# The feed-forward of the L2 attention by pairs of sequences, and the keys and values of the L3 attention made early and kept in DRAM

## The chip, the cores and the metric

The kernel is one program on one core of a Trainium2 chip. Its engines run side by side, each through its own queue in order: PE (TensorE, the matmuls; PEld are its weight loads), DVE (VectorE), ACT (ScalarE), POOL (GpSimd) and SP (SyncE, which here only starts DMA transfers). An engine waits for another by semaphores. The metric is the device time of the program in microseconds (us), lower is better, and a comparison goes by the median of several runs.

## The reference, cut to what matters

The input x holds 8 sequences of 128 rows and 128 channels in fp32; ctx_1024 holds 77 context rows for each sequence. Eight blocks are added to x one after the other: L0_xattn, L0_ffn, L1_xattn, L1_ffn (64 routed experts, the best 3 for each row), L2_xattn, L2_ffn (six layers of windowed local attention), L3_xattn, L3_ffn (two such layers). The change touches these three:

```python
x = x + _L1_ffn_ref(_layernorm(x), ...)                     # experts
# L2_xattn: 16 heads of 8 channels, then a feed-forward of 512, both with a norm behind them
q, k, v = query @ Wq + bq, context @ Wk + bk, context @ Wv + bv
o = softmax(rope(q) @ rope(k).T / sqrt(8)) @ v @ Wo + bo
x = _layernorm(query + o, g1, b1)
ff = relu(x @ W1 + bf1) @ W2 + bf2
x = _layernorm(x + ff, g2, b2)
...
# L2_ffn, each of six layers: shift, QKV, norm of q and k, rotation, windowed softmax, Wo, gated feed-forward
# L3_xattn: 8 heads of 64 channels; y is the context, so k and v depend on no layer before it
xn = _layer_norm(x, ln_scale, ln_bias)
q, (k, v) = xn @ Wq, split(y @ Wkv)
out = softmax(q @ k.T / 8) @ v @ Wo
```

A sequence depends on no other sequence in all of this (only the routing of the experts looks across them).

## The kernel before, in words

The program has two parts, each a list of steps that a planner in the program's builder puts in order. A step names the engines that may do it with a guessed time for each, the tiles it reads and writes, and the kind of buffer it opens ("big" is 128x512 fp32, "row" 128x128, "mm" one of the 8 PSUM banks). `Plan.arranged` (line 599) plays the steps through with these guesses and writes down for each engine a fixed order; on the chip only this order and the semaphores are left. A step may be picked only while its rank is less than 600 (`AHEAD`) above that of the first step not yet started; steps of SP are free of this limit (line 639). So which tile a buffer number holds, and where an instruction stands in its queue, is decided by the planner.

**The front part** (`plan_front`, line 971) holds L0, L1_xattn and the experts. SP loads the packs of weights first and then, as 51 big buffers allow (`BUFS_A`, line 966), the weights of the 64 experts, 128 tiles of 256 KB, 38 of them before it has to wait for the routed rows (`rows_in`, line 1380), 90 behind them. Each expert's result goes to DRAM (`expert_ys`).

**The later part** (`plan_later`, line 2038) begins with the gathers: for each of the 8 sequences POOL starts three indirect transfers out of `expert_ys` (line 1464) and DVE adds each to x with its gate (line 1469). Behind them `one(b)` (line 1538) does the L2 attention of one sequence: a norm (DVE statistics L775 and L777; four POOL instructions L768, L782, L783, L784 for the root; ACT L792), a transpose (L754), two projections and a rotation (L761, L1501, L1505), scores (L847), exponentials (L855), sums and outputs (L863), a reciprocal (L869), the projection (L883, L884) and the sum `y` (L1550).

`layer(h)` (line 1555) then does the feed-forward of L2_xattn for a half, four sequences at once: norm, the affine step on POOL (`affine`, L1601 and L1602), transposes, four matmuls of 512 columns (L761) with ReLU (L1572 on ACT or L1574 on DVE), 4x5 small matmuls (L1582, L1584), a sum (L1588), a second norm and affine step, and the sum into x on POOL (L1594). `begin(l2, h)` (line 1690) makes the normed input `y_res` of the local layers for these four.

A local layer (class `Local`) takes one sequence at a time. `first` makes the shifted transposed input `hs` of a half (`shifted`, line 1743) and then queries and keys: matmuls L1757, the rotation on DVE (L1779, L1781, L1783) and POOL (L1784, L1797), the inverse root with Ln and Exp on ACT (L1810, L1811). `rest` does the attention (scores L1862 and L1868, exponentials L1875, sums and outputs L1923 and L1929, Ln and Exp again at L1883 and L1884, projection L1843, sum into `y_res` L1847). `gated` (line 1938), a gated feed-forward over a half, ends a layer: it opens with a matmul that shifts rows (L1944), goes on with L1961, L1974 and L1984, and leaves ACT with the table of Ln and Exp together (`preload_act_table_set`, L1969).

The order in which `plan_later` writes the steps: `one` for sequences 0 to 3; the loads of the first local weights and of the pack `w3`, all held behind the gathers of sequence 3 (`route.behind(3, ...)`); `layer(0)`, `begin(l2, 0)`; then `one` for 4 to 7 side by side with the first local layer of 0 to 3; `layer(1)`, `begin(l2, 1)`, `gated(l2, 0, 0)`, and so on, half by half through six layers. Beside the local attention of the last half-layers stands L3_xattn (`plan_xattn_64`, line 1605): for each half four matmuls make the transposed keys (128 context columns of four sequences, 308 columns), and for each sequence one matmul makes the values (77x512), all from `ctxT` and the part `L3_kv` of the pack `w3`. Each result is copied out of PSUM into a big buffer (L741 on ACT, L743 on DVE).

At the very end a flag decides by a branch whether a slower general version must run; here it never does.

Of the kernel before, what the change touches and what calls it, by code (L numbers as in the profile page):

```python
# [25 lines left out]
B = 8  # L26
# [109 lines left out]
def laid_out(i):  # L136
# [54 lines left out]
    w3.add("L3_kv", i["L3_xattn_Wkv"])  # L191
    w3.add("L3_o", chunked(i["L3_xattn_Wo"]))

    def local(m, qkv, wo, a, b):
        rest = [np.concatenate([chunked(o), with_unit(u), chunked(padded_rows(np.concatenate([d, e[None]]), 3 * P))], 1)
                for o, u, d, e in zip(i[m + wo], i[m + a], i[m + b], i[m + "b2"])]
# [12 lines left out]
        "wg": wg.array(), "w": w.array(), "w3": w3.array(),  # L209
# [4 lines left out]
                    "w": w.at, "w3": w3.at}  # L214
# [5 lines left out]
class Chip:  # L220


    def __init__(self, ctx, tc, a, at):
# [8 lines left out]
        for name in ("col", "row", "cst", "wg", "w"):  # L232
            self.room(name, self.keep)
# [290 lines left out]
class Step:  # L524
    def __init__(self, rank, ns, emit, mode, tail, spare):
        self.rank, self.ns, self.emit, self.mode, self.tail, self.spare = rank, ns, emit, mode, tail, spare
        self.wants, self.gives, self.vals, self.opens = 0, [], [], []
        self.ready, self.start, self.engine = 0.0, None, None


class Plan:
# [32 lines left out]
    def add(self, ns, emit, reads=(), writes=(), mode=None, opens=(), tail=None, spare=0):  # L564


        s = Step(len(self.steps), ns, emit, mode, tail, spare)
# [31 lines left out]
    def arranged(self):  # L599
# [22 lines left out]
        while times:  # L622
# [8 lines left out]
            for e in free:  # L631
# [3 lines left out]
                while came[e]:  # L635
                    rank, s = heapq.heappop(came[e])
                    if s.start is not None:
                        continue
                    if (rank < first + self.AHEAD or e == "SP") and held.isdisjoint(v.tag for v in s.opens) and open_to(s):
                        pick = s  # L640
                        break
                    tags = [v.tag for v in s.opens]
                    held.update(k for k in ("mm",) if tags.count(k) > 1)
                    kept.append((rank, s))
# [321 lines left out]
BUFS_A = {"tiny": 30, "few": 3, "row": 6, "big": 51, "huge": 3, "w": 1, "wr": 1}  # L966
# [4 lines left out]
def plan_front(w, early, dram, wide, narrow):  # L971
# [41 lines left out]
    pack("w", 3000)  # L1013
    for e in range(EARLY):
        route.weights(e)
# [517 lines left out]
def plan_l2_xattn(w, ctx, route):  # L1533
# [21 lines left out]
    def layer(h):  # L1555
        xs, y = w.xs[4 * h : 4 * h + 4], [ys[4 * h + j] for j in range(4)]
        y1 = w.tile([P, 4, P])
        w.normed(lambda k, y1=y1: y1()[:, k, :], lambda k, y=y: y[k](), y, [y1])
        affine(w, y1, "L2_xattn_g1", "L2_xattn_b1")
        yT = w.tile([P, 4, P])  # L1560
        tp = w.turn(lambda k, y1=y1: y1()[:, k, :], [y1])
        w.copy(yT, tp, [tp], [yT], 591, 682)
        hs = []
        for k in range(4):
            ps, hT = w.bank([P, 4 * P]), w.tile([P, 4 * P])
            w.mm(ps, lambda k=k: c.get("w", "L2_W1", k * P, P), lambda yT=yT: yT().rearrange("p b s -> p (b s)"), [yT], [ps],
                 860)
# [8 lines left out]
            plan.add({"ACT": 597, "DVE": 683}, relu, [ps], [hT])  # L1576
            hs.append(hT)
        out, y2 = w.bank([P, 4, P]), w.tile([P, 4, P])
        for j in range(4):
# [8 lines left out]
        plan.add({"DVE": 683}, lambda e, y1=y1, y2=y2, out=out: nc.vector.tensor_tensor(y2(), y1(), out(), ALU.add),  # L1588
                 [y1, out], [y2])
        y3 = w.tile([P, 4, P])  # L1590
        w.normed(lambda k, y3=y3: y3()[:, k, :], lambda k, y2=y2: y2()[:, k, :], [y2], [y3])
        affine(w, y3, "L2_xattn_g2", "L2_xattn_b2")
        xv = c.x[:, 4 * h : 4 * h + 4, :]
        plan.add({"POOL": 1270}, lambda e, y3=y3, xv=xv: nc.gpsimd.tensor_tensor(xv, xv, y3(), ALU.add), [y3, *xs], xs)  # L1594
# [4 lines left out]
def affine(w, v, g, b):  # L1599
    c, nc = w.c, w.c.nc  # L1600
    w.plan.add({"POOL": 1270}, lambda e: nc.gpsimd.tensor_tensor(v(), v(), spread(c.get("row", g), 4, 1), ALU.mult), [v], [v])  # L1601
    w.plan.add({"POOL": 1270}, lambda e: nc.gpsimd.tensor_tensor(v(), v(), spread(c.get("row", b), 4, 1), ALU.add), [v], [v])  # L1602


def plan_xattn_64(w, nch, wq, wkv, wo, gamma, beta, bias, finish):
# [12 lines left out]

    def group(h, g, xT):
        qTs, kTs = [], []  # L1620
        for k in range(4 * g, 4 * g + 4):
            ps, kT = w.bank([P, 4, KC]), w.tile([P, 4, KC])
            w.mm(lambda ps=ps: ps().rearrange("p b k -> p (b k)"), lambda k=k: wkv[:, k * P : (k + 1) * P],
                 lambda: c.ctxT[:, h * 4 * KC : (h + 1) * 4 * KC], [], [ps], 520, opens=[kT])
            w.copy(kT, ps, [ps], [kT], 430, 470)
            kTs.append(kT)
# [14 lines left out]
        for j in range(4):  # L1641
            b = 4 * h + j
            ps, v = w.bank([KC, 512]), w.tile([KC, 512])
            w.mm(ps, lambda b=b: c.ctxT[:, b * KC : (b + 1) * KC],
                 lambda: wkv[:, inner + g * 512 : inner + (g + 1) * 512], [], [ps], 860, opens=[v])
            w.copy(v, ps, [ps], [v], 591, 682)
            finish(b, w.attend_64(qTs, j * P, kTs, j, v, wo[:, 4 * g : 4 * g + 4, :],
# [4 lines left out]
    return half  # L1652


def plan_l3_xattn(w):
    c, nc = w.c, w.c.nc

    def finish(b, out):
# [3 lines left out]
    return plan_xattn_64(w, 4, c.get("w3", "L3_q"), c.get("w3", "L3_kv"), c.get("w3", "L3_o").rearrange("p (c d) -> p c d", d=P),  # L1662
                         c.get("col", "L3_xattn_ln_scale"), c.get("col", "L3_xattn_ln_bias"), None, finish)


AHEAD = 1
BUFS_C = {"w": 2, "wr": 2, "tiny": 24, "few": 12, "row": 20, "big": 48}


class Local:  # L1670
# [4 lines left out]
    def __init__(self, w, name, depth, nch, window, wa, wb, room, wo=None):  # L1675
# [12 lines left out]
        self.layers, self.hs, self.begun = {}, {}, {}  # L1688

    def begin(self, h):  # L1690
        at = slice(4 * h, 4 * h + 4)
        self.w.normed(lambda k: self.y[:, 4 * h + k, :], lambda k: self.c.x[:, 4 * h + k, :], self.w.xs[at], self.ys[at])

    def first(self, l, h, j):
# [3 lines left out]
        if j == 0:  # L1698
            self.hs[h] = self.shifted(h)
        self.begun[l, h, j] = self.queries_keys(self.layers[l], self.hs[h], j)  # L1700

    def rest(self, l, h, j):

        self.attention(self.layers[l], 4 * h + j, self.hs[h], j, *self.begun.pop((l, h, j)))
# [38 lines left out]
    def shifted(self, h):  # L1743

        nc, plan = self.c.nc, self.plan
        hs = self.tile([P, 4, P])
        y = self.y
        tp = self.turn(lambda k: y[:, 4 * h + k, :], self.ys[4 * h : 4 * h + 4])
        plan.add({"POOL": 150}, lambda e: nc.gpsimd.memset(hs()[64:128, :, 0:1], 0.0), [], [hs])
        self.copy(lambda: hs()[0:64], lambda: tp()[0:64], [tp], [hs])  # L1750
        self.copy(lambda: hs()[64:128, :, 1:P], lambda: tp()[64:128, :, 0 : P - 1], [tp], [hs])
# [286 lines left out]
def plan_later(w, route, l2x, l2, l3x, l3, stored):  # L2038


    order = [(loc, l, h, j) for loc, depth in ((l2, 6), (l3, 2)) for l in range(depth) for h in range(2) for j in range(4)]
# [3 lines left out]
    def some(n):  # L2045

        for i in range(n):
            while at["first"] < min(at["rest"] + 1 + AHEAD, len(order)) and order[at["first"]][:3] in given:
                loc, l, h, j = order[at["first"]]
                loc.first(l, h, j)  # L2050
                at["first"] += 1
            loc, l, h, j = order[at["rest"]]
            loc.rest(l, h, j)
# [13 lines left out]
    def begin(loc, h):  # L2067
        loc.begin(h)
        given.add((loc, 0, h))

    def gated(loc, l, h):
        loc.gated(l, 4 * h, 4)
        given.add((loc, l + 1, h))

    one, layer = l2x
    side_by_side(each(one, range(4)))

    behind = lambda load: route.behind(3, load)
    l2.layers[0] = l2.weights(0, [w.xs[3]], behind)
# [118 lines left out]
```

## Time and profile before

| what | us |
|---|---|
| three runs without the profiler | 1550.05, 1552.71, 1555.53 (median 1552.71) |
| the profiled execution, its own device time | 1561.18 |
| its span, first to last instruction | 1559.4 |
| PE busy / DVE / ACT / POOL | 1425.1 / 920.4 / 936.9 / 816.6 |
| last matmul of the experts ends | 395.3 |
| first gather starts / last gather starts | 398.4 / 449.5 |
| first matmul of the local layers (L1757) | 486.9 |
| first L1944 (layer 0, first half) / second L1944 (second half) | 571.7 / 653.1 |
| keys of L3_xattn: first half / second half | 1238.6 to 1242 / 1315.4 to 1318 |

How to read it: the profile gives for each engine its busy time and what ended each idle stretch in front of an instruction; for PE also the clock that was granted, as a part of full speed. The stage that the change is about lies between 395 and 653 us, the time from the end of the experts to the moment when all 8 sequences have their first local layer's attention behind them. A view of "windows" gives each engine's busy time in a stretch that one chooses, with the count of its instructions; a "timeline" gives them one after the other.

### The profile page before, as it was taken

Reading aid. Unit: us, or ns where it says so; the run is one execution under the profiler, and the core shown is the slowest. Engines: PE = TensorE matmul, PEld = TensorE weight load, DVE = VectorE, ACT = ScalarE, POOL = GpSimd, SP = SyncE. Lnnn points to the kernel's source line nnn. Section 1 sums busy time; section 2 is a strip of 40 time slices with the busy share of each in tenths; the row PEclk is TensorE's granted clock in tenths of the full one; section 3 lists DMA queues with packets and bytes.
Section 4 is the critical chain, followed back from the end, with each engine's and each line's share of the span. In section 5 each row is a group of like instructions: output and inputs, shape, how many; then the busy total and the mean of one; then the engine's idle time right before and its main releaser. Section 6 shows DMA issues by size and latency. Waiting matters only on the chain.

```text
span 1559.4 us, 39024 instructions
## 1 busy us (share of the span) xinstructions
PE 1425.1 (91%) x16007; PEld 972.3 (62%) x16007; DVE 920.4 (59%) x1995; ACT 936.9 (60%) x1917; POOL 816.6 (52%) x1243
## 2 busy tenths in 40 slices
PE   7999998598587869999999999999999999899996
PEld 4777775375363555675666766667666667475654
DVE  5543764523356428668577585766857665657563
ACT  3676564253245846666666666666666676566764
POOL 3310225310566727777595674956749572536561
PEclk7999999699697989999999999999999999999997
DMA  9300001388301000100100010010000000000000
GB/s 335 131 1 21 8 2 42 111 296 324 124 21 69 1 1 1 56 16 2 42 16 15 2 56 16 1 49 23 2 22 22 2 22 2 21 2 1 1 2 16
DMA packets 39964, 74.00 MB, mean 47 GB/s; under 512 B 4102, under 2 KB 18630, under 8 KB 38496
## 3 DMA queue, kind: packets, MB, share of 16 engines
q1 hardware_dynamic: 33888, 66.16, 12.3%
q0 software_dynamic: 1536, 3.15, 0.6%
q8 instruction: 128, 2.10, 0.5%
q10 hardware_dynamic: 4352, 2.10, 0.5%
q14 instruction: 60, 0.49, 0.1%
HBM read 65.10 MB, written 6.29 MB: 46 GB/s over the span
## 4 chain that ended last, share of the span: by engine, by line
PE 59%; DVE 19%; ACT 8%; POOL 7%; issue 4%; DMA 2%; another core or an unknown queue 0%; ACTq 0%; SPq 0%; POOLq 0%; DVEq 0%
PE mm L1757 8%; PE mm L754 7%; PE mm L761 5%; PE mm L1843 5%; DVE big L1779 4%; DVE big L1781 4%; DVE few L1783 4%; PE mm L1868 3%; PE mm L1929 3%; PE mm L1984 3%; PE mm L1961 2%; PE mm L1974 2%; PE mm L863 2%; PE mm L1189 2%; PE mm L1175 2%
## 5 line engine op out<-in xcount | busy, mean ns | idle before, releaser
L741 ACT COPY big<-mm 128x512 f32<-128x512 f32 (+4 forms) x512 | 276.4, 565 | 222.0 <-PE mm L754 118.0
L1784 POOL TENSOR_TENSOR big<-big,big 128x512 f32<-128x512 f32 x224 | 283.8, 1275 | 237.1 <-DVE big L1781 232.0
L1757 PE MATMUL mm<-wide,big 128*128 128x512 f32 x672 | 323.5, 611 | 13.1 <-ACT big L741 10.6
L1797 POOL TENSOR_TENSOR big<-big,few 128x512 f32<-128x512 f32 x224 | 226.8, 1042 | 1.6
L754 PE MATMUL mm<-ident,big 128*128 128x128 f32 (+1 forms) x1430 | 206.4, 280 | 19.5 <-ACT big L792 4.4
L754 PEld LDWEIGHTS mm<-ident,big 128*128 128x128 f32 (+1 forms) x1430 | 162.7, 143 | 96.8 <-POOL big L1797 31.9
L1757 PEld LDWEIGHTS mm<-wide,big 128*128 128x128 f32 x672 | 120.0, 194 | 116.3 <-issue 83.9
L1779 DVE TENSOR_TENSOR big<-mm,big 128x512 f32<-128x512 f32 x224 | 152.4, 680 | 64.0 <-ACT big L1778 61.0
L1778 ACT ACTIVATE big<-mm 128x512 f32<-128x512 f32 x224 | 133.0, 597 | 91.0 <-PE mm L1757 83.5
L1781 DVE TENSOR_TENSOR big<-mm,big 128x512 f32<-128x512 f32 x224 | 152.4, 680 | 5.3 <-ACT big L1778 5.3
L1783 DVE TENSOR_REDUCE few<-big 128x8 f32<-128x512 f32 x224 | 151.0, 674 | 6.5 <-ACT big L1778 6.5
L1875 ACT ACTIVATE big<-mm 128x512 f32<-128x512 f32 x224 | 118.2, 610 | 34.4 <-PE mm L1868 34.4
L1843 PE MATMUL mm<-narrow,big 128*128 128x128 f32 x896 | 117.2, 283 | 11.6 <-DVE big L1891 11.3
L1843 PEld LDWEIGHTS mm<-narrow,big 128*128 128x128 f32 x896 | 108.6, 196 | 28.3 <-DVE big L1891 17.9
L1885 DVE TENSOR_TENSOR mm<-mm,big 128x512 f32<-128x512 f32 x64 | 44.5, 696 | 132.0 <-ACT big L1884 130.5
L1929 PEld LDWEIGHTS mm<-big,big 128*32 128x32 f32 x3072 | 86.7, 110 | 27.9 <-issue 27.2
L1868 PE MATMUL mm<-big,big 64*64 64x64 f32 (+2 forms) x3584 | 100.4, 238 | 1.2 <-ACT big L741 1.2
L1868 PEld LDWEIGHTS mm<-big,big 64*64 64x64 f32 x3584 | 94.2, 133 | 6.3 <-ACT big L741 2.0
L1929 PE MATMUL mm<-big,big 128*32 128x128 f32 x3072 | 94.1, 273 | 0.1
L822 POOL TENSOR_TENSOR big<-big,tiny 128x308 f32<-128x308 f32 x40 | 27.9, 700 | 97.3 <-DVE tiny L819 47.2
L1891 DVE SCALAR_TENSOR_TENSOR big<-mm,big 128x512 f32<-128x512 f32 x112 | 73.1, 686 | 5.6 <-PE mm L1929 0.4
L743 DVE COPY big<-mm 77x512 f32<-77x512 f32 (+2 forms) x74 | 47.6, 656 | 29.7 <-PE mm L1189 9.1
(277 smaller groups left out, 2335.4 us busy)
## 6 DMA issues: line engine op xcount, KB each, us to landing
big<-in_experts_dram SPq DMA_DIRECT2D x128, 256.0 KB, 4.9
wide<-in_l2a_dram SPq DMA_DIRECT2D x6, 1536.0 KB, 6.6
narrow<-in_l2b_dram SPq DMA_DIRECT2D x6, 534.0 KB, 3.5
narrow<-in_l2o_dram SPq DMA_DIRECT2D x6, 512.0 KB, 3.6
p_w<-in_w_dram SPq DMA_DIRECT2D x1, 2048.0 KB
expert_rows<-big SPq DMA_DIRECT2D x8, 256.0 KB, 13.9
big<-expert_rows SPq DMA_DIRECT2D x8, 256.0 KB, 3.8
expert_ys<-big ACTq DMA_DIRECT2D x16, 128.0 KB, 4.3
```

The source lines that it names most:

```text
L741: nc.scalar.copy(out(), in_())
L754: nc.tensor.transpose(tp()[:, k, :], v(k), c.ident)
L1757: self.plan.add({"PE": 860}, lambda e: nc.tensor.matmul(ps(), lhsT=hs()[:, j, :], rhs=wqkv()[:, o : o + 512], start=True, stop=True), [hs, ...
L1778: yield lambda e: nc.scalar.activation(sq(), heads(), AF.Square)
L1779: yield lambda e: nc.vector.tensor_tensor(t1(), heads(), spread(rot()[:, 2 * kind, :], 8, 1), ALU.mult)
L1781: yield lambda e: nc.vector.tensor_tensor(halves(t2()), halves(heads())[:, :, ::-1, :], sin(), ALU.mult)
L1783: yield lambda e: nc.vector.tensor_reduce(ss()[:, lo : lo + 8], sq(), AX.X, ALU.add)
L1784: yield lambda e: nc.gpsimd.tensor_tensor(t1(), t1(), t2(), ALU.add)
L1797: plan.add({"POOL": 1062}, lambda e, t=t, t1=t1, i=i: nc.gpsimd.tensor_tensor(t(), t1(), spread(r()[:, 8 * i : 8 * i + 8], 64, 2), ALU.mul ...
L1843: nc.tensor.matmul(out(), lhsT=oT()[:, k, :], rhs=wo()[:, 4 * g + k, :], start=(g == 0 and k == 0), stop=(4 * g + k == nch - 1))
L1868: nc.tensor.matmul(sc[s]()[at : at + 64, k, q:end], lhsT=kT()[lo : lo + 64, k, at : at + 64], rhs=qT()[lo : lo + 64, k, q:end], start=Fals ...
L1929: nc.tensor.matmul(avs[half]()[32 * t : 32 * t + 32, k, :], lhsT=vs[t // 2]()[:, at : at + 32], rhs=prs[t]()[:, k, :], start=True, stop=True)
```

## The change

Four things are done, all by the order and the size of steps; the sums computed are the same.

1. `layer` and `begin` work on any run of sequences, and `plan_later` calls them for pairs: `one` for 0 and 1, `layer` and `begin` for 0 and 1, then 2 and 3, and so on. In the first local layer the shifted input too is made by pairs. All four pairs stand before the first local attention in the written order, and `gated(l2, 0, 0)` stands behind the attention of all of sequences 0 to 3 as before.
2. The 8 key and 8 value tiles of L3_xattn are made at the start of the later part (`ahead`), written to 16 DRAM tiles (`Kept.put`, behind the gathers of sequence 1) and read back into big buffers where L3_xattn needs them (`Kept.get`). The reads may be started up to 300 ranks ahead (`within`).
3. The part `L3_kv` becomes a pack of its own, `w3kv` (128x1024, 512 KB), which stays in SBUF from the front part on and is loaded there before the experts' weights; the front's big buffers go from 51 to 49 for it.
4. The loads of the first local weights and of `w3` are held behind the gathers of sequence 1 and not 3.

```diff
-BUFS_A = {"tiny": 30, "few": 3, "row": 6, "big": 51, "huge": 3, "w": 1, "wr": 1}
+BUFS_A = {"tiny": 30, "few": 3, "row": 6, "big": 49, "huge": 3, "w": 1, "wr": 1}
...
     pack("w", 3000)
+    pack("w3kv", 1700)
     for e in range(EARLY):
         route.weights(e)
...
-    def layer(h):
-        xs, y = w.xs[4 * h : 4 * h + 4], [ys[4 * h + j] for j in range(4)]
-        y1 = w.tile([P, 4, P])
+    def layer(b0, n):
+        xs, y = w.xs[b0 : b0 + n], [ys[b0 + j] for j in range(n)]
+        y1 = w.tile([P, n, P])
...
+def affine(w, v, g, b, n):
+    nc = w.c.nc
+    for name, op in ((g, ALU.mult), (b, ALU.add)):
+        w.plan.add({"POOL": 80 + 300 * n}, lambda e, name=name, op=op: nc.gpsimd.tensor_tensor(
+            v(), v(), spread(w.c.get("row", name), n, 1), op), [v], [v])
...
+    def keys(h, k):
+        ps, kT = w.bank([P, 4, KC]), w.tile([P, 4, KC])
+        w.mm(lambda: ps().rearrange("p b k -> p (b k)"), lambda: wkv[:, k * P : (k + 1) * P],
+             lambda: c.ctxT[:, h * 4 * KC : (h + 1) * 4 * KC], [], [ps], 520, opens=[kT])
+        w.copy(kT, ps, [ps], [kT], 430, 470)
+        return kT
+
+    def values(b, g):
+        ps, v = w.bank([KC, 512]), w.tile([KC, 512])
+        w.mm(ps, lambda: c.ctxT[:, b * KC : (b + 1) * KC], lambda: wkv[:, inner + g * 512 : inner + (g + 1) * 512], [], [ps],
+             860, opens=[v])
+        w.copy(v, ps, [ps], [v], 591, 682)
+        return v
+
+    def ahead():
+
+        return [v for h in range(2) for v in (*(keys(h, k) for k in range(nch)), *(values(4 * h + j, 0) for j in range(4)))]
...
+class Kept:
+
+
+    def __init__(self, w, dram, name, n):
+        self.w, self.rooms, self.there = w, [dram.tile([P, 512], F32, name=f"{name}{i}") for i in range(n)], []
+
+    def put(self, vs, after, begun):
+        for v, room in zip(vs, self.rooms):
+            there = self.w.plan.fixed(None)
+            n = lambda v=v: int(np.prod(v().shape[1:]))
+            self.there.append(there)
+            self.w.plan.add({"SP": 500}, lambda e, v=v, room=room, n=n: begun(
+                self.w.c.nc.sync.dma_start(room[: v().shape[0], 0 : n()], self.flat(v()))), [v, *after], [there])
...
+    def get(self, shape, i):
+        v = self.w.tile(shape)
+        self.w.plan.add({"SP": 500}, lambda e: self.w.c.nc.sync.dma_start(
+            self.flat(v()), self.rooms[i][: shape[0], 0 : int(np.prod(shape[1:]))]), [self.there[i]], [v], within=300)
+        return v
...
-    one, layer = l2x
-    side_by_side(each(one, range(4)))
-
-    behind = lambda load: route.behind(3, load)
-    l2.layers[0] = l2.weights(0, [w.xs[3]], behind)
-    w.plan.add({"SP": 5000}, lambda e: behind(w.c.load("w3")), [w.xs[3]], [])
-    layer(0)
-    begin(l2, 0)
-    side_by_side(each(one, range(4, 8)), some(4))
+    (one, layer), (l3x, ahead, kept) = l2x, l3x
+    ahead = ahead()
+    for k in range(4):
+        side_by_side(each(one, (2 * k, 2 * k + 1)))
+        if k == 0:
+
+            behind = lambda transfer: route.behind(1, transfer)
+            kept.put(ahead, [w.xs[1]], behind)
+            l2.layers[0] = l2.weights(0, [w.xs[1]], behind)
+            w.plan.add({"SP": 5000}, lambda e: behind(w.c.load("w3")), [w.xs[1]], [])
+        layer(2 * k, 2)
+        begin(l2, 2 * k, 2)
+    side_by_side(some(4))
     plan_flag(w)
-    layer(1)
-    begin(l2, 1)
     gated(l2, 0, 0)
```

## The prediction

> **What bounds the kernel now.** I read the busy shares by slice first, then windows at the edges of the stage that is edited, then the chain of waits and single instructions there.
>
> ```profile
> PE   7999998598587869999999999999999999899996
> PEclk7999999699697989999999999999999999999997
> ...
> 395.30:408.90 13.60, 0.00 (x0) 0.00 (x0) 3.49 (x11) 0.86 (x2) 8.25 (x12) 0.55 0.15 43
> ...
> 486.90:571.70 84.80, 71.78 (x800) 47.51 (x800) 43.60 (x80) 60.00 (x95) 48.07 (x66) 0.93 0.01 1
> 571.70:600.00 28.30, 21.70 (x68) 11.42 (x69) 16.52 (x40) 14.84 (x28) 11.94 (x21) 0.82 0.00 1
> 600.00:653.10 53.10, 52.50 (x763) 37.04 (x762) 36.38 (x62) 36.45 (x73) 45.35 (x63) 1.00 0.09 32
> 653.10:1238.00 584.90, 580.58 (x7145) 387.17 (x7147) 406.22 (x732) 394.78 (x758) 394.64 (x543) 1.00 0.06 20
> 1238.00:1316.00 78.00, 76.73 (x1041) 53.80 (x1030) 45.36 (x99) 52.29 (x115) 42.55 (x65) 1.00 0.04 12
> 1316.00:1344.70 28.70, 24.01 (x129) 14.80 (x128) 14.18 (x41) 16.05 (x34) 8.27 (x15) 0.94 0.08 29
> ```
>
> Behind the length of a window stand the busy times of PE, PEld, DVE, ACT and POOL, then PE's clock and the DMA share. From 600 to 1316 PE is busy over 98% at full clock: there the time is PE's work, and whatever work PE is relieved of, or has done sooner, comes off the end. From 395.3 (the experts' last matmul) to 653.1 (the second L1944) PE is idle for 51.9 of 257.8 us, and part of the rest runs at a lower clock. That stage is bound by waits:
>
> ```profile
> 398.42 1.01 POOL row L1464
> ...
> 447.78 1.05 POOL tiny L782
> 449.48 1.09 POOL row L1464
> ...
> 480.00 1.04 POOL tiny L782
> 481.90 1.04 POOL tiny L782
> 484.01 1.64 PE mm L754 x4
> 486.89 9.83 PE mm L1757 x20
> 497.35 1.28 ACT L1810
> 498.89 1.28 ACT L1811
> ```
>
> These are pieces of the chain: gathers and roots on POOL, one feed-forward of four sequences from 444 to 487 in which PE has little beside it, then local attention that needs Ln and Exp in turn, each time with a table load of 1.28 us on ACT.
>
> **The landmark.** I compared the order in which the changed program issues its instructions. From the experts' end to the second L1944 its PE queue holds what it held, with W1 split into twice as many matmuls of half the width, plus the 16 matmuls for keys and values; behind it, only these 16 are missing. So the change is worth (a) the shift of the second L1944, (b) the missing work after it, (c) side costs. The sum is made against the profiled execution, 1561.2 us (span 1559.4); that is 8.5 us or 0.5% above the median of the runs, 1552.7, and I take the same difference off both.
>
> **Keys and values, early.** Eight matmuls of 308 columns, 0.52 us apart at 1315.4 to 1316.4, and eight of 512 columns, 0.86 apart: 8 x 0.52 + 8 x 0.86 = 11.0 us of PE. They now stand first in the later part, in the 13.6 us before 408.9 when PE does nothing, so they cost nothing there. ACT takes 14 of the 16 copies, 13 of them ahead of the first norm of sequence 0: about 13 x 0.5 = 6.5 us, and ACT is busy 0.86 us of that gap. If the cover were short by two matmuls, the first transposes would come 1.7 us late. Taken: 0.
>
> **Keys and values, gone later (b).** Those of the first half and the first values stand between 1238.6 and 1307, where PE is 98% busy: 5.5 us come off. The other 5.5 stand at 1315 to 1326, but there the gated feed-forward follows a chain of its own (L1944 at 1316.4, L1961 only at 1329.0, behind an idle PE): between 0 and 5.5, taken 1 because the chain is the nearer row. Together -6.5.
>
> **POOL up to the first local matmul.** POOL is nearly the serial resource here, so I counted its queue from the first gather to the root for pair 0's `y_res`, at start-to-start times of the trace: 24 gathers x 1.25 = 30.0, eight one-column roots x 1.4 = 11.4, four two-column ones x 1.6 = 6.3 (between 1.4 and the 1.9 of four columns), five watches x 1.06, seven L1505 x 0.52, six affine halves x 0.65, rotation tables 1.5, a residual and memsets 1.1: 63.4 us. In the kernel before, the same count to the half's root is 69.4 and took 398.4 to 483.4, a fill of 0.82. At that fill: 398.4 + 63.4 / 0.82 = 476; then two scalings, a transpose and two copies, 2.4 us against 3.5 for four sequences: first L1757 at 478 instead of 486.9. Full POOL would give 464.
>
> **From there to the second L1944.** At full clock the PE work of this stretch was 71.78 x 0.93 + 21.70 x 0.82 + 52.50 = 137 of 166.2 us: 29 lost. The changed order leaves the last sequence's L2 attention behind the first L1757, about 4 us, so 141. With nothing lost: 478 + 141 = 619; with 29 lost: 648. More stands beside the waits now: in the changed order, 12 projections of later sequences and 24 transposes stand ahead of the first L1944 that stood behind it. The row for a stage with sequences to spare is 600 to 653, which loses 0.6; the row for the same chain is the one that loses 29. I take half, 14.5: 633.5. POOL's queue to this point grows from 179.7 to 189.2 us (six more roots, affine steps by halves). From 478 it has 125.8 left; at a fill of 0.80, between 0.71 for the whole stage before (179.7 / 254.7) and 0.85 for 600 to 653, this ends at 635. Both say about 634: -19 (a). ACT gets eight more table loads before the first gated step, 8 x 1.28 = 10.3 us; PE waits for ACT there, and I count them inside the 14.5.
>
> The next loads' users start at once in the trace (load at 497.35, ACTIVATE at 498.65). The Trainium skill's page "ScalarE: Activation LUTs", section "What ACT_TABLE_LOAD costs", speaks against the change: a switch of tables costs the load of about 1283 ns and some 1380 ns of drain. By the page's 2.66 us the eight would be an estimated 21 us; the trace shows the first half alone, since nothing stands between a load and its user.
>
> **Front part (c).** The pack of keys and values moves ahead of the experts' weights; 36 instead of 38 expert tiles can be fetched early. Half a MB more at 391 GB/s (370 to 380 us) is 1.3 us in a stretch in which PE waits for weights in part; the weights end at 382, PE 13 us later. Between 0 and 1.5, taken +1.
>
> **DMA during the gathers (c).** SP now has 16 writes of 154 KB (2.5 MB) ahead of the local weights, all released behind sequence 1's gathers instead of 3's: 5.7 MB instead of 3.7 (with `w3`), at the 359 GB/s of 420 to 430 about 16 us instead of 10. In those, gathers landed some 3 us later than the 2.5 of the first. SP queues the local weights behind the writes; they are due at 478 and land by about 430. Gathers of later pairs have attention of earlier ones in front of them, so between 0 and 3 us: +1. The 16 reads back have SP to themselves: before, it waits from 1078 to 1130 and from 1201 to 1273. Twelve of them stand ahead of the L3 weights, which were in place at 1135 and are needed at 1338; each waits only for its buffer. Cost 0; with the cover gone, 4 us of a 768 KB load.
>
> **Sum:** -19 - 6.5 + 1 + 1 = -23.5; against the runs 1552.7 - 23 = **1530 us**.
>
> **Rivals.**
> *The attention chain sets the pace.* Ln and Exp in turn, with their loads, cost what they cost and pairs add eight: loss 29 + 10.3, the second L1944 at 478 + 141 + 39.3 = 658. Then +5 - 6.5 + 2, near 1553. For it: of the waits at 484 to 600 the longest is DVE on ACT's L1884, 24.1 us. Against it: other sequences' projections are in the queue by then. Chance 0.17, from 1546 to 1558: a third of it faster, half within the noise.
> *POOL becomes the bound, and the kernel is slower.* It gets 9.5 us more, and each root stands in order behind gathers whose data it awaits. If its fill stays 0.71 the second L1944 comes at 398.4 + 189.2 / 0.71 = 665: +12 - 6.5 + 2 = +7.5, 1560. It decides from a fill below 0.73 (second L1944 at 657.6). For it: its idle time there is made by waits for DVE's L1781 (18.5 us from 484 to 600) and L1501 (10.2 from 398 to 484). Against: 0.85 where sequences are plentiful. Chance 0.09.
> *PE is bound almost from the first gather.* The K/V matmuls hold the clock, POOL runs full and 4 us are lost: 464 + 141 + 4 = 609, -44 - 7.5 + 1, near 1502. Chance 0.05.
> *The stores and reads hurt elsewhere* (gathers late one behind the other, or the L3 weights held up): 3 us for each of three pairs on top, 1539. Chance 0.06.
>
> **How the numbers follow.** The forecast has 0.63, with 1516 to 1544 of its own (POOL's fill behind 478 from 0.88 to 0.74). The range of 8 in 10 runs from 1512 to 1553: below it lies the full-PE case, above it the slower one and the upper part of the chain case, 0.05 + 0.09 + 0.06 left out. A measurement can tell about 0.3%, 4.7 us. Faster: 0.63 + 0.05 + 0.06 and 0.06 of the chain case, 0.80; within 0.3%: 0.08 of the chain case; slower: 0.09 + 0.03, 0.12.
>
> **What would show it.** Right: L761 with `w3kv` in the gap after the experts; first L1757 at 470 to 480 and second L1944 at 625 to 645 of the span, PE's clock 1 by 415; no such matmuls after 1200. Wrong: POOL busy over 85% from 400 to 650 with PE waiting for it; a late DVE L1469 in a row; PE idle behind ACT table loads as before; an L1757 of L3 waiting for DMA. A second L1944 above 658 ends the forecast.

## The result, and the profile after

| | median us | range | runs |
|---|---|---|---|
| before (the three runs above and three taken with the changed kernel) | 1557.89 | 1550.05 to 1565.98 | 6 |
| changed | 1540.53 | 1539.38 to 1542.45 | 6 |

The ratio is 0.9877, 95% interval 0.9849 to 0.9905: 1.2% faster, some 19 us (17.4 between the medians). The forecast was -23 us, 1530. The two sets of runs of the kernel before lie apart themselves: the three above have a median of 1552.7, the three taken with the changed kernel 1562.5. In the profiled executions the span went from 1559.4 to 1538.4 us. The lines below are those of the page for the changed kernel: the busy shares, and 40 slices of 38 us for PE and its clock.

```profile
span 1538.4 us, 39251 instructions
PE 1428.4 (93%) x16023; PEld 981.0 (64%) x16023; DVE 918.5 (60%) x1988; ACT 952.8 (62%) x1948; POOL 823.7 (54%) x1279
PE   7999998598789888999999999999999999899996
PEclk7999998699779998999999999999999999999998
```

The edited stage is in the slices 11 to 17. PE goes from 5 to 7 tenths in the first of them and is at 8 or 9 in the others. The same in windows (length, then the busy times of PE, PEld, DVE, ACT, POOL, then PE's clock and the DMA share); the edges are the experts' end, the first transpose behind the gathers, the first L1802 (the line that was L1757), the first and second L1989 (was L1944), and two in the last layers:

```profile
388.70:402.60 13.90, 11.29 (x34) 5.21 (x33) 4.10 (x12) 7.05 (x16) 8.81 (x17) 1.00 0.21 62
402.60:471.30 68.70, 59.36 (x808) 49.44 (x809) 30.30 (x104) 30.55 (x68) 48.68 (x103) 0.70 0.28 97
471.30:576.30 105.00, 91.50 (x967) 60.18 (x966) 62.91 (x128) 83.67 (x143) 78.47 (x125) 0.95 0.07 27
576.30:643.60 67.30, 61.58 (x781) 41.85 (x780) 37.73 (x69) 44.36 (x78) 36.70 (x54) 0.92 0.07 25
643.60:1228.00 584.40, 580.38 (x7145) 387.07 (x7147) 405.90 (x732) 394.82 (x758) 394.75 (x543) 1.00 0.06 19
1228.00:1302.00 74.00, 71.65 (x1024) 51.45 (x1016) 46.52 (x102) 50.11 (x116) 43.89 (x67) 1.00 0.17 56
```

Against the kernel before, the parts of the way are:

| stretch | before | changed | forecast of the difference |
|---|---|---|---|
| start to the experts' end | 395.3 | 388.7 | about +1 |
| experts' end to first local matmul | 91.6 | 82.6 | -8.9 |
| from there to the second gated step (L1944, now L1989) | 166.2 | 172.3 | -10.7 |
| from there to the end of the span | 906.3 | 894.8 | -6.5 |

So the first local matmul came forward by what was forecast, but two thirds of that was given back before the second gated step. The total came near the forecast because the first row and the last row gave more than they were expected to. Both had to be explained before the total could count as understood.

The keys and values lie where the forecast put them. PE's timeline of the changed kernel behind the experts (start, duration, line, tile sizes, count; each of the 16 matmuls has two records):

```profile
388.68 2.37 PE L763 MATMUL mm<-ctxT_sb,p_w3kv 128*128 128x308 f32 x8
390.89 3.60 PE L763 MATMUL mm<-p_w3kv,ctxT_sb 128*77 128x512 f32 x8
394.32 2.24 PE L763 MATMUL mm<-ctxT_sb,p_w3kv 128*128 128x308 f32 x8
396.39 3.60 PE L763 MATMUL mm<-p_w3kv,ctxT_sb 128*77 128x512 f32 x8
402.60 0.33 PE L756 MATMUL mm<-ident,row 128*128 128x128 f32 x1 [2.61 <-ACT row L794]
```

The first transpose of the later part comes 13.9 us behind the experts' last matmul, as in the kernel before (13.7): in its place the 11 us cost nothing.

What gave the time back is on ACT, as `after_tables` below shows. Its timeline inside the third window, with one sequence's local attention:

```profile
504.97 1.28 ACT L1855 ACT_TABLE_LOAD   x1
506.27 0.23 ACT L1855 ACTIVATE few<-few 128x32 f32<-128x32 f32 x1
506.51 1.28 ACT L1856 ACT_TABLE_LOAD   x1
507.81 0.23 ACT L1856 ACTIVATE few<-few 128x32 f32<-128x32 f32 x1
507.94 1.06 ACT L1920 ACTIVATE big<-mm 128x512 f32<-128x512 f32 x2
509.02 1.28 ACT L1928 ACT_TABLE_LOAD   x1
510.32 0.60 ACT L1928 ACTIVATE big<-mm 128x512 f32<-128x512 f32 x1
510.93 1.28 ACT L1929 ACT_TABLE_LOAD   x1
512.23 0.63 ACT L1929 ACTIVATE big<-big 128x512 f32<-128x512 f32 x1
```

Ln (L1855, L1928) and Exp (L1856, L1929) follow each other, and each first loads a table of 1.28 us for an instruction of 0.23 or 0.6 us. Four loads belong to one sequence. The waits of the same stage (471 to 644 us; waiting engine and line, what it waited for, total, times, longest) put this chain first:

```profile
DVE mm L1930 <- ACT big L1929: 40.0, 6, 10.6
POOL few L1859 <- ACT few L1856: 26.4, 9, 8.0
```

The loads end with the first gated step, which leaves a table with both functions on ACT. Before it the order has four sequences' Ln and Exp by halves (4 x 4 = 16 loads); by pairs it has those for the norms of seven sequences and for the sums of five (7 x 2 + 5 x 2 = 24). The same table is also asked for when the later part begins, but that load stands outside the plan and lands at the very start of the program, 390 us before it would be of use (the row below). Other loads follow in the front part; the last two ahead of the local layers are the experts' Gelu (L1437, at 310.4) and the first Exp of the L2 attention (L857, at 406.0).

```profile
0.72 1.28 ACT L2171 ACT_TABLE_LOAD   x1 [0.72 <-PEq L2237]
```

### The profile page after: what moved, and what is told of

Same layout as the page of the kernel before. It is cut to its first block, busy times and chain, and to the rows that moved or that the text cites. A ratio compares the mean times of both kernels' runs of the same rounds, so it can differ in the third digit from the quotient of the medians.

```text
span 1538.4 us, 39251 instructions
## 1 busy us (share of the span) xinstructions
PE 1428.4 (93%) x16023; PEld 981.0 (64%) x16023; DVE 918.5 (60%) x1988; ACT 952.8 (62%) x1948; POOL 823.7 (54%) x1279
## 4 chain that ended last, share of the span: by engine, by line
PE 56%; DVE 17%; POOL 12%; ACT 8%; issue 4%; DMA 2%; POOLq 0%; SPq 0%; DVEq 0%; ACTq 0%
PE mm L756 8%; PE mm L1802 7%; PE mm L763 4%; PE mm L1888 4%; DVE big L1824 4%; DVE big L1826 4%; DVE few L1828 4%; PE mm L1974 3%; PE mm L2029 3%; PE mm L2006 3%; PE mm L1913 3%; PE mm L2019 2%; POOL big L1842 2%; POOL big L1829 2%; PE mm L1192 2%
## 5 line engine op out<-in xcount | busy, mean ns | idle before, releaser
L743 ACT COPY big<-mm 128x512 f32<-128x512 f32 (+6 forms) x521 | 278.7, 559 | 224.4 <-PE mm L756 136.1
L1802 PE MATMUL mm<-wide,big 128*128 128x512 f32 x672 | 319.8, 602 | 9.1 <-ACT big L743 9.1
L1842 POOL TENSOR_TENSOR big<-big,few 128x512 f32<-128x512 f32 x224 | 227.2, 1043 | 1.6
L1802 PEld LDWEIGHTS mm<-wide,big 128*128 128x128 f32 x672 | 118.1, 192 | 105.8 <-issue 80.0
L1888 PEld LDWEIGHTS mm<-narrow,big 128*128 128x128 f32 x896 | 108.6, 196 | 24.9 <-DVE big L1936 13.7
```

The costliest lines, as they stand in the source:

```text
L743: nc.scalar.copy(out(), in_())
L1802: self.plan.add({"PE": 860}, lambda e: nc.tensor.matmul(ps(), lhsT=hs()[:, j, :], rhs=wqkv()[:, o : o + 512], start=True, stop=True), [hs, ...
L1842: plan.add({"POOL": 1062}, lambda e, t=t, t1=t1, i=i: nc.gpsimd.tensor_tensor(t(), t1(), spread(r()[:, 8 * i : 8 * i + 8], 64, 2), ALU.mul ...
L1888: nc.tensor.matmul(out(), lhsT=oT()[:, k, :], rhs=wo()[:, 4 * g + k, :], start=(g == 0 and k == 0), stop=(4 * g + k == nch - 1))
```

## The experiments

They ran in three groups of four kernels, each group on another chip, with the kernel before timed beside them (median 1560.4 of 17 runs, 1562.0 of 23, 1563.0 of 11). Ratios are to those runs.

### The two parts alone

`after_again` is the changed kernel unedited.

> The changed kernel once more, to see which differences between the first two profiles return. In the first two, the experts' last matmul ended 6.5 us earlier in the changed kernel (388.7 instead of 395.25), though my sum had +1 there. Theory (scatter between executions): the ratio stays at 0.985 to 0.991 and the experts' end falls anywhere from 385 to 397. Rival (the front part really is shorter): the experts' end is again at 388 to 390. Distance from the experts' end to the second L1989 again 253 to 257 us under both.

`pairs_only` takes the early keys and values out:

```diff
-BUFS_A = {"tiny": 30, "few": 3, "row": 6, "big": 49, "huge": 3, "w": 1, "wr": 1}
+BUFS_A = {"tiny": 30, "few": 3, "row": 6, "big": 51, "huge": 3, "w": 1, "wr": 1}
...
-    pack("w3kv", 1700)
...
-    ahead = ahead()
...
-            kept.put(ahead, [w.xs[1]], behind)
...
-                   plan_l3_xattn(w, Kept(w, dram, "kept", 16)),
+                   plan_l3_xattn(w),
```

> Only the pairs: the last attention's keys and values are made where the kernel before makes them, their weights lie in w3 again, 51 big buffers in the front. Theory (the pairs bring the first local matmul 9 us forward, and the first local layer's attention chain with 24 table loads gives nearly all of it back; the early keys and values cost nothing): from the experts' end to the second gated step's L1944 253 to 256 us instead of 257.8, and -2 to -5 us in all, ratio 0.997 to 0.999. Rival 1 (the early keys and values cost 5 to 8 us in the gathers, which hid a larger gain from the pairs): 246 to 250 us, -8 to -12, ratio 0.992 to 0.995. Rival 2 (the earlier fetch of the keys' weights shortens the front part): experts' end at 394 to 396 here.

`kv_only` puts the halves back:

```diff
-    for k in range(4):
-        side_by_side(each(one, (2 * k, 2 * k + 1)))
...
-        layer(2 * k, 2)
-        begin(l2, 2 * k, 2)
-    side_by_side(some(4))
+    side_by_side(each(one, range(4)))
+    behind = lambda transfer: route.behind(3, transfer)
+    kept.put(ahead, [w.xs[3]], behind)
...
+    layer(0, 4)
+    begin(l2, 0, 4)
+    side_by_side(each(one, range(4, 8)), some(4))
     plan_flag(w)
+    layer(4, 4)
+    begin(l2, 4, 4)
```

> Only the keys and values: made first in the later part, written to DRAM behind the gathers of sequence 3, read back; feed-forward and first local input by halves of four sequences as before. Theory (11 us of PE work filled an idle gap and are missing at 1230 to 1330, where PE is the bound in both halves): experts' end to the second L1944 257 to 260 us, and -10 to -12 us in all, ratio 0.992 to 0.994; with a front part that is really 6 us shorter (rival 2) -17, ratio 0.989. Rival 1 (not free in the gathers): 262 to 266 us, and -3 to -6, ratio 0.996 to 0.998.

Measured (to the first local matmul and to the second gated step from the experts' end; the last column from the second gated step to the end):

| kernel | ratio, interval | experts' end | to first local | to 2nd gated | behind it |
|---|---|---|---|---|---|
| after_again | 0.9887, 0.9866 to 0.9908 | 390.7 | 82.1 | 254.2 | 898.8 |
| pairs_only | 0.9919, 0.9900 to 0.9939 | 386.0 | 80.8 | 252.1 | 906.3 |
| kv_only | 0.9922, 0.9894 to 0.9950 | 389.1 | 92.9 | 258.1 | 899.2 |

The keys and values came out as the theory had it: nothing in the gathers (258.1 against 257.8), 7 us behind. The pairs did not: the trace gives them 5.7 us in their stage and nothing behind it, the runs gave 12.6. In the profiles the rest lies ahead of the experts' end (386.0 against 395.3), where this kernel issues the same instructions as the kernel before. Its 252.1 us lie between theory and rival 1; against rival 1 stand the 258.1 us of `kv_only`, in which the early keys and values cost nothing there, and the 258.1 of `pairs_again` below. The early end also rules out rival 2, since this kernel has no early pack and has the earliest experts' end of all.

### Is the front part shorter, or does it scatter?

`before_again` is the kernel before unedited, `pairs_again` the pairs alone, unedited.

> The kernel before once more, against itself. Up to the experts' end the changed kernel, both halves of it and the kernel before issue nearly the same instructions, and the one with only the pairs issues exactly the same as the kernel before; yet the experts' last matmul ended at 395.3 in the kernel before and at 386.0 to 390.7 in the four profiles of the others. Theory A (scatter between executions, from the granted clock and the first loads): ratio 0.997 to 1.003 and an experts' end at 386 to 392 this time. Theory B (the front part is really slower in this program): again at 393 to 397. From the experts' end to the second L1944 257 to 259 us, and 905 to 908 us from there to the end, under both.

> Only the pairs, once more. Its six runs lay at 1546.6 to 1548.4, 13.5 us below the kernel before, while its profile shows only 5.7 us from the edited stage (252.1 against 257.8 us) and nothing behind it (906.3 us in both); the other 9 lie ahead of the experts' end, in instructions that are the same. Theory A (scatter): experts' end at 386 to 395, ratio 0.990 to 0.997. Theory B (the program's own): again at 385 to 388, ratio 0.990 to 0.993.

The experts' last group of matmuls (PE's timeline; its last matmul ends 1 us later), first in `pairs_only`, then in `pairs_again`, which is the same program, then in `before_again`:

```profile
384.90 1.09 PE L1443 MATMUL mm<-big,big 128*64 128x128 f32 x16 [0.48 <-ACT big L1435]
```

```profile
394.38 1.09 PE L1443 MATMUL mm<-big,big 128*64 128x128 f32 x16 [0.48 <-ACT big L1435]
```

```profile
391.07 1.09 PE L1442 MATMUL mm<-big,big 128*64 128x128 f32 x16 [0.48 <-ACT big L1434]
```

One program gives 386.0 and 395.5. Over all 14 profiles the experts' end lies between 386.0 and 395.5; the seven with the early pack have a mean of 390.4, the seven without it 391.4. So the front part scatters by up to 10 us, and the first row of the table above says nothing of the change. `before_again` had a ratio of 0.9998 (0.9974 to 1.0023). `pairs_again` had 0.9963 (0.9941 to 0.9985), 258.1 us to the second gated step and 906.0 behind it: on this chip the pairs alone brought 6 us by the runs, on the other 13. The edited stage scatters too: one program took 252.1 and 258.1 us for it. Theory A held, with `pairs_only` a fortunate draw; why its runs in one group lie 7 us beside those in the other stays open.

### The table loads

`after_tables` asks for the joint table inside the plan, just ahead of the first Exp of the later part. The order of the other instructions on ACT, DVE and POOL is the same in both traces; the table loads in the trace go from 79 to 55, by the 24 ahead of the first gated step. (An expectation below speaks of 90 loads that are left; the traces have 55.)

```diff
+        self.primed = False
...
-            plan.add({"ACT": 597}, lambda e, pr=pr, t=t: nc.scalar.activation(pr(), sc[t](), AF.Exp), [sc[t]], [pr])
+            def exps(e, pr=pr, t=t):
+                if self.norms_on_act and not self.primed:
+                    self.primed = True
+                    nc.scalar.preload_act_table_set("natural_log_exp_and_others")
+                nc.scalar.activation(pr(), sc[t](), AF.Exp)
+
+            plan.add({"ACT": 597}, exps, [sc[t]], [pr])
```

> The changed kernel with one load of the table that has Ln and Exp together just ahead of the first Exp of the L2 attention, inside the plan: the 24 loads between there and the first gated step are gone (24 x 1.283 = 30.8 us of ACT), and nothing else in any engine's order changes. Theory (the chain through ACT and its loads is what gave the 9 us back): from the first L1802 to the second L1989 155 to 162 us instead of 172.3, in all 10 to 17 us less than the changed kernel, ratio to the kernel before 0.977 to 0.982. Rival (POOL, which has 9.5 us more to do there, is the bound): 169 us or more, under 4 us gained, ratio 0.985 to 0.989. Rival (ACT's loads lie where DVE or PE wait for something else anyway): no change either.

Ratio 0.9717 (0.9690 to 0.9744), median 1516.52 us: 26 us less than the changed kernel beside it, more than the 10 to 17 expected. Windows of `after_tables` from its first local matmul to its first and second gated step, to be laid beside the third and fourth window of the changed kernel:

```profile
468.40:553.80 85.40, 83.11 (x967) 54.89 (x966) 62.77 (x128) 58.41 (x123) 78.47 (x125) 1.00 0.09 33
553.80:613.75 59.95, 57.45 (x781) 40.56 (x780) 37.75 (x69) 38.92 (x74) 36.59 (x54) 1.00 0.08 28
```

172.3 us have become 145.3, where 155 to 162 were expected. ACT is busy 97.3 instead of 128.0 us, 30.7 less, which is 24 x 1.283; POOL is busy as before (115.1 and 115.2), so POOL was not the bound. PE's idle time goes from 19.2 to 4.8 us, and its busy time from 153.1 to 140.6 for the same matmuls, while the granted clock goes from 0.95 and 0.92 to 1.00. So of the 27 us some 14 were PE waiting, and some 12 are matmuls that took longer; the lower clock accounts for about 9.5 of these (153.1 - 143.6, the busy times times their clocks). Both rivals are out: taking 31 us of loads away brought 27. The wait that was 40.0 us is shorter, and now without loads in it (waits of `after_tables`, same stage):

```profile
DVE mm L1937 <- ACT big L1936: 25.4, 6, 6.1
```

`before_tables` is the same edit in the kernel before (16 loads gone, 71 in the trace become 55).

> The kernel before with the table that has Ln and Exp together loaded once ahead of the first Exp of the L2 attention: its 16 table loads between there and the first gated step are gone (16 x 1.283 = 20.5 us of ACT). Theory (the loads lie on the chain that PE waits for, in halves as in pairs, as the 24 of the changed kernel did at 26 of 31 us): from the first L1757 to the second L1944 146 to 152 us instead of 166.2, and 14 to 20 us less in all, ratio 0.987 to 0.991. The pairs are then worth what they bring the first local matmul forward: about 10 us between this kernel and the changed one with the same load. Rival (in halves the loads lie beside other work): under 8 us, ratio above 0.995.

Ratio 0.9908 (0.9881 to 0.9935). From the first local matmul to the second gated step 153.0 us, 13 less than 166.2 and just outside the 146 to 152 expected. All of it comes ahead of the first gated step, 71.5 us instead of 84.8; the windows of `before_tables` to the first and second gated step:

```profile
485.17:556.68 71.51, 68.19 (x800) 46.11 (x800) 43.52 (x80) 40.48 (x79) 47.98 (x66) 0.96 0.01 2
556.68:638.18 81.50, 74.31 (x829) 48.45 (x829) 52.87 (x101) 51.29 (x100) 57.27 (x83) 0.94 0.06 21
```

So 20.5 us of loads cost 13 in halves, and 30.8 cost 27 in pairs. The expectation's last sentence, some 10 us between this kernel and the changed one with the same load, did not hold: in the square below it is 25.8.

### Is POOL the bound ahead of the first local matmul?

`tables_affine` is `after_tables` with the affine steps and the residual of the feed-forward open to DVE:

```diff
-        w.plan.add({"POOL": 80 + 300 * n}, lambda e, name=name, op=op: nc.gpsimd.tensor_tensor(
+        w.plan.add({"POOL": 80 + 300 * n, "DVE": 145 + 134 * n}, lambda e, name=name, op=op: (nc.vector if e == "DVE" else nc.gpsimd).tensor_tensor(
...
-        plan.add({"POOL": 80 + 300 * n}, lambda e, y3=y3, xv=xv: nc.gpsimd.tensor_tensor(xv, xv, y3(), ALU.add), [y3, *xs], xs)
+        plan.add({"POOL": 80 + 300 * n, "DVE": 145 + 134 * n}, lambda e, y3=y3, xv=xv: (nc.vector if e == "DVE" else nc.gpsimd).tensor_tensor(xv, xv, y3(), ALU.add), [y3, *xs], xs)
```

> The changed kernel with the one table load, and with the scaling, the bias and the residual of the feed-forward's norms free to go to DVE as well as POOL: 14 of the 20 half-size steps go to DVE, 14 x 0.65 = 9 us less on POOL up to the second gated step. Theory (POOL's queue sets when the first local matmul can start, about five of these steps lie ahead of it): first local matmul 77 to 80 us behind the experts' end instead of 81.6, the second gated step's L1989 at 221 to 225 instead of 227, ratio to the kernel before 0.968 to 0.971. Rival (POOL only waits for others there): 81 to 83 and 226 to 229, ratio 0.971 to 0.974.

Ratio 0.9749 (0.9719 to 0.9778). The first window is that of `after_tables`, the second that of `tables_affine`, both from the experts' end to the first local matmul:

```profile
386.80:468.40 81.60, 67.00 (x842) 51.39 (x841) 34.67 (x115) 37.32 (x83) 57.58 (x119) 0.79 0.28 92
```

```profile
393.80:476.20 82.40, 69.14 (x872) 52.36 (x870) 38.41 (x127) 35.96 (x79) 54.81 (x112) 0.79 0.28 92
```

POOL had 2.8 us less to do here, and the first local matmul came no earlier (82.4 against 81.6). That is the rival's figure; the second gated step, 229.6 us behind the experts' end, and the ratio lie just beyond its ranges. So nothing shows that POOL's queue sets this point. But the test is not a clean one: the edit changed the planned order as well, and PE has 30 more matmuls ahead of the first local one (872 against 842), DVE 12 more instructions.

### The square without the loads

All four corners in one group, each with the one table load. `before_tables_again` and `after_tables_again` are as above; `pairs_tables` and `kv_tables` are `pairs_only` and `kv_only` with the edit of `after_tables`.

> The kernel before with the one table load, once more, as the first corner of a square in one call: neither part, pairs, keys and values, both, all four with the 90 table loads that are left in each. Its first run gave 0.991, with the first local matmul 97.4 us behind the experts' end (91.6 and 93.3 in the two profiles of the kernel before, whose instructions are the same up to there), in a stretch with the clock at 0.73. Expected under every theory: ratio 0.986 to 0.993, from the first local matmul to the second L1944 150 to 154 us.

> Only the pairs, with the one table load (24 loads gone). Theory (the forecast's shift of the second gated step, -19 us, was hidden by the eight loads that the pairs add and by the chain that they lie on): from the experts' end to the second gated step 226 to 234 us, against 245 to 250 for the kernel before with the same load; 16 to 21 us less than that kernel, where without the load the pairs brought 6 to 13. Rival (the pairs' gain needs the early keys and values, which keep PE and its clock up in the gap): 236 to 242 us, under 12 us less.

> Only the keys and values, with the one table load (16 loads gone). Theory (their worth lies behind the second gated step and does not depend on the loads): from there to the end 897 to 900 us instead of 906, from the experts' end to there as in the kernel before with the same load, 245 to 251; 6 to 10 us less than that kernel. Rival (they take the place of idle time that the loads leave): under 3 or over 14.

> Both parts with the one table load, the fourth corner. Theory: the two parts add up, 23 to 30 us less than the kernel before with the same load, ratio to the kernel before 0.969 to 0.975; from the experts' end to the second gated step 225 to 232 us. Without the load the same sum was -18 of the kernel before.

| kernel | median us | ratio, interval | to first local | to 2nd gated | behind it |
|---|---|---|---|---|---|
| before_tables_again | 1547.05 | 0.9892, 0.9863 to 0.9922 | 92.4 | 244.5 | 907.0 |
| pairs_tables | 1530.66 | 0.9783, 0.9756 to 0.9810 | 83.0 | 227.2 | 905.4 |
| kv_tables | 1540.12 | 0.9847, 0.9817 to 0.9878 | 96.5 | 248.9 | 899.2 |
| after_tables_again | 1521.22 | 0.9721, 0.9696 to 0.9745 | 82.7 | 228.2 | 904.4 |

Now the pairs bring 16.4 us by the medians and 17.3 in their stage. The keys and values bring 6.9 alone and 9.4 on top of the pairs, both parts together 25.8. The windows of `pairs_tables` from the experts' end show that they need no early keys for it:

```profile
388.45:471.50 83.05, 55.98 (x845) 45.35 (x843) 34.65 (x117) 30.67 (x67) 58.53 (x121) 0.75 0.20 67
471.50:555.75 84.25, 80.90 (x934) 54.00 (x933) 63.20 (x128) 56.15 (x122) 77.19 (x124) 1.00 0.09 33
555.75:615.70 59.95, 57.14 (x782) 40.66 (x781) 37.74 (x69) 38.90 (x74) 36.87 (x54) 1.00 0.08 28
```

The theory held at all four corners, with one miss: the last column of `after_tables_again` is 904.4, though `after_tables` had 897.0. The two part only from the gated step at 1276 us on, in layers that are the same; PE's clock is 0.93 from there to the end, against 0.96 over the same layers in `after_tables`. The instructions being the same, this too is scatter.

## Why the prediction was right, and where it was not

The total came out near the forecast, the parts only in part, and some of the nearness is luck.

**The landmark** held. What the order comparison said, that nothing but the 16 matmuls differs behind the second gated step, is seen in the time from there to the end: 905.4 to 907.0 us in all seven profiles with late keys and values, pairs or not. PE's records there are 10006 in the kernel before and 9974 in the changed one, 32 fewer for the 16 matmuls.

**Keys and values early, 0**: held. With the loads gone, the second gated step of the pairs is reached after 226.9 and 228.2 us with them and 227.2 without. In halves it is 248.9 with them, 244.5 and 250.4 without, which is no sign of a cost beyond the scatter.

**Keys and values gone later, -6.5**: held. The seven profiles with them early have a mean of 899.1 from the second gated step to the end, the seven others 906.3: -7.2. The split was right as well. At the gated step at 1300 us the difference of the means is 6.3 (forecast 5.5 for the first half), and only some 0.7 is added up to the next one (forecast 1 of 5.5): the second half's matmuls lay beside a chain. The -11.5 of the first pair of profiles is a draw of 894.8 from a spread of 894.8 to 904.4.

**First local matmul, 478 at an experts' end of 395.3, that is 82.7 us behind it**: held, 80.8 to 83.6 in eight profiles with pairs. The reasoning behind it, POOL's queue at a fill of 0.82, is not shown: `tables_affine` took POOL work away and moved nothing, though in another order of steps. The clock was misjudged too. It was to be full by 415; from 402.6 to 450 us it was about 0.6 (the windows below), and from 430 to 450 PE was busy 19.7 of 20 us at it.

**From there to the second gated step, 141 us of work and "half of before's 29 us loss"**: this step failed. The work was right (91.50 x 0.95 + 61.58 x 0.92 = 143.6), but the loss stayed whole: 172.3 - 143.6 = 28.7 us. The eight added loads, 10.3 us, were counted inside the 14.5, as if other sequences' projections would cover them. The loads are not covered: with all 24 out, PE is idle for 4.8 of 145.3 us, at full clock. The other working of this term, POOL's queue ending at 635, fails with it: POOL was as busy without the loads, in 27 us less. In ACT's timeline above a load starts 0.01 us behind the instruction before it and its user starts 0.02 us behind the load; ACT's busy time fell by 1.28 us for each load, the stage by 27 for 24. The Trainium skill's page "ScalarE: Activation LUTs", section "What ACT_TABLE_LOAD costs", would add some 1380 ns of drain to each load; this trace does not show it.

So (a) was -3.6 (mean of two profiles each: 254.5 against 258.1, with 252.1 and 258.1 for the pairs alone) and not -19. The mechanism was that of the rival "the attention chain sets the pace", which had a chance of 0.17, and the sign of being wrong that the prediction named, PE idle behind table loads as before, was there. The rival overpriced it, with a loss of 29 + 10.3. The runs part the two effects in this stretch: without the loads the pairs shorten it by 7 to 8 us (153.0 and 152.0 against 145.3, 144.2 and 145.5), but with them in it the loads cost 27 instead of 13, so it came out 6 us longer. From the experts' end the pairs bring 17 us once the loads are out, near the 19 forecast.

That the second gated step was at 643.6 us, inside the 625 to 645 named as a sign of being right, is luck: the experts ended 6.5 us earlier in this profile, and from their end it took 254.9 us, where 238.2 were forecast (633.5 - 395.3).

**The front and the transfers, +1 each**: not to be told from a scatter of 10 us. DVE's waits for gathers did grow with the early keys and values (L1469, now L1472: 14.7 us in the kernel before, 23.5 in the changed one, 23.3 in `kv_only`), but the first local matmul came no later for it, and no L1802 waited for a transfer.

**The sum.** The traces support -3.6 - 7.2 = -11 for the change, the runs gave -19 and -18, with intervals from -24 to -14. The difference of the first two profiles, -21, has -6.5 in the front part and 4 in the draw behind the second gated step. Why the medians lean the same way is open. Four programs were timed in two groups each: three had ratios within 0.0016 of each other, the pairs alone differed by 0.0044, 7 us. So the total came within some 5 us of the forecast although (a) fell short by 15 in the traces: 7 or 8 us of what was measured lie in no part that these traces explain.

The version that beats both kernels is the changed one with one table load in its place: 0.9717 and 0.9721 of the kernel before, 0.983 (0.9717 / 0.9887) of the changed one.

## What to carry to other kernels

When a change brings work forward into a chain, price the chain's own fixed costs first; a load of 1.28 us ahead of an instruction of 0.23 us was visible in the timeline of before, and taking it out was worth more than the change. A setting that is issued outside the scheduled list of steps lands where the builder stands, not where the reader sees it: look for it in the engine's queue. And compare landmarks relative to the start of the edited stage, and over two profiles, before a difference ahead of the stage is given a cause.

## What was not expected of the hardware

PE's clock sags to about 0.6 behind the experts, whether PE has work in the gap or not (0.64 from 408.9 to 430 us in the kernel before). Windows of the changed kernel through the gathers, right behind 14 us at full clock:

```profile
402.60:415.00 12.40, 8.66 (x120) 7.49 (x124) 3.46 (x12) 6.69 (x14) 10.21 (x18) 0.58 0.83 273
415.00:430.00 15.00, 12.63 (x168) 10.71 (x164) 8.94 (x32) 4.00 (x10) 10.81 (x23) 0.61 0.50 188
430.00:450.00 20.00, 19.67 (x201) 16.01 (x193) 8.66 (x31) 6.92 (x17) 13.37 (x29) 0.61 0.08 20
450.00:471.30 21.30, 18.40 (x336) 15.23 (x336) 9.23 (x32) 12.94 (x30) 14.30 (x36) 0.92 0.01 3
```

The early keys and values did not hold the clock up, as the rival "PE is bound almost from the first gather" had it. From 430 to 450 PE is 98% busy at 0.61, so in a stretch that looks full the work takes an estimated half as long again or more (1 / 0.61). From the experts' end to the first local matmul the mean clock is 0.71 to 0.84 in all 14 profiles, and each of them has a stretch of 7 us, within 100 us of the experts' end, with PE at least 90% busy and the clock at 0.50 to 0.55. What sets this is not shown. And the waits behind the table loads cost more than PE's idle time shows: of the 27 us that taking the loads out brought, 14 were idle time; most of the rest goes with the clock, 0.92 to 0.95 instead of 1.00 over 172 us.
